# Two attention-convolution layers: the weight bands of layer 0 in one transfer per image, and the loads of x on another queue

## The chip, the cores and the metric

The kernel runs on one core of a Trainium2 chip. Its engines are TensorE (PE), VectorE (DVE), ScalarE (ACT), GpSimd (POOL) and SyncE (SP). SP and ACT each have a queue through which they issue DMA transfers; both queues feed the same 16 DMA engines. An engine works through its own instructions in order, and a DMA issue stands in that order like any other instruction: if it has to wait, everything behind it on that engine waits too. The metric is the device time of one execution in microseconds, as the median of several runs.

## The reference

The input x is 8 images of 56 x 56 pixels with 384 channels in float32. Two layers follow each other, each with a residual, and everything is float32.

```python
# layer 0, per image; gn = group norm with 32 groups, no affine part
xn = gn(x)
v = xn @ Wv.T                                       # 384 -> 384
a = (xn @ Wa.T).reshape(n, 12 heads, 9, 9)          # 384 -> 972
attn = softmax(a * 32 ** -0.5, axis=-1)
out[n, p, head] = sum over q of attn[n, head, p, q] * v[neighbour q of n, head]
y = fold(out)             # out[.., p] is added at neighbour p of its pixel
x = x + y @ Wo.T
# layer 1
xn = gn(x)
a = softmax((xn @ W_attn + b_attn).reshape(n, 6 heads, 9), axis=-1)
v = xn @ W_v + b_v
y[n, head] = sum over k of a[n, head, k] * v[neighbour k of n, head]
x = x + y @ W_proj + b_proj
```

Neighbours are the 3 x 3 pixels around one, and outside the image v is zero. In layer 0 each pixel gathers from 9 neighbours with 9 sets of weights and scatters the 9 results onto its neighbours, so altogether a pixel of y depends on the v of 5 x 5 pixels.

## The kernel before

Two images make a pair: R = 112 rows (both images' rows) lie on the partitions, and the work walks over the 56 columns. In layer 0 a step is one column of one pair, 224 steps in all, and a group is PX = 7 columns (NPX = 8 groups for each of 4 pairs).

What a step of layer 0 does. `attend` projects the column's normalised pixels to the 972 logits in three parts on TensorE, subtracts the maximum on DVE, takes the exponential on ACT (L491), sums and inverts on DVE, and normalises on POOL. It also projects v for a tile of 128 pixels, copies it on ACT (L498) and writes it to the table `vtab0` in DRAM through ACT's queue (`spread`, L296). `presum` and `fold` add up the weights that meet at the same pair of pixels, so that gathering and scattering together become one 5 x 5 stencil; `fold` copies the result (L555, L556) and writes it to one of three tables `ztab0` in DRAM through ACT's queue (L561).

The tables turn the stencil into matrix products. For a patch of 7 x 7 target pixels the 11 x 11 source pixels are the contraction, so 121 partitions. `rows_to_patches` (L361) reads v of these pixels from `vtab0` into `vp`, and `bands` (L308) reads the weights from `ztab0` into `z`, a tile of 128 partitions (source pixels) by 8 patches by 7 rows of targets. The table is skewed so that a plain strided read yields the matrix: row s of `z` begins a slot further on in the table, and where a source pixel is too far from a row of targets, the read meets the zeros with which the tables were filled before (`clear_weights`). For one image `z` is a band matrix: the first 48 source pixels reach only the first five of seven rows of targets, the last ones only the last four. `GROUPS0` (L88) splits the partitions into three ranges and gives each its rows of targets, and `bands` issues one transfer for each range. `z` is zeroed once at the start, so what no range reads stays zero. `contract` then multiplies `vp` and `z` on TensorE head by head and copies the result `pc` to `yT` on ACT (L600); `project_out` multiplies by Wo, adds the residual `xres`, and sends the result to DRAM.

The order of this work. `fetch_v` and `fetch` are called once for each group and issue the loads of `vp`, `z` and `xres` on SP; their contractions and projections go into a list of jobs that later steps run, from four steps on, two jobs a step. The order of TensorE's products is the order of the program, and a list scheduler of the compiler orders the other engines. Besides, `upkeep` runs in every step. It prepares the statistics of the next pair: `stats_load` reads four columns of x into `xr` (L392), `stats_chunk` transposes them on TensorE three steps later (L122), copies them on ACT (L409), takes sums on DVE and stores the transposed block to `xT` (L413). It also loads the transposed blocks of the present pair: `load` reads one into `xin` (L460), and four steps later `normed` normalises it on ACT (L471). `xr` and `xin` have two buffers each. The first pair's statistics come before all this, in a loop of their own at the start.

DMA completions are told by eight semaphores that the two queues share: a transfer that reuses one waits until that semaphore's last transfer has landed.

Layer 1 works in the same way with 3 x 3 stencils; its bands are read with `GROUPS1`, and its loads are issued by SP.

Of the kernel before, what the change touches and what calls it, by code (L numbers as in the profile page):

```python
# [15 lines left out]
def two_outlook_layers(  # L16
# [32 lines left out]
    nc = tc.nc  # L49

    B, H, W, C = x.shape
    P = 128
    NCH = C // P
    IMG = 2
    R = IMG * H
# [7 lines left out]
    XB = 4  # L63
# [21 lines left out]
    PY1, NPY1, SX1, SY1 = 8, 7, PX + 2, 10  # L85
    ROW1 = HEADS1 * PX

    GROUPS0 = (((0, 48), (0, 5)), ((48, 80), (0, 7)), ((80, P), (3, 7)))  # L88
    GROUPS1 = (((0, 45), (0, 5)), ((45, 90), (3, 8)))


# [8 lines left out]
    xf = x.rearrange("b y x c -> (b y) x c")  # L100
# [132 lines left out]
    def norm_params(st, name, params, key):  # L233

        mv = stat.tile([P, NCH, IMG, 2], F32, tag="mv", name=f"mv_{name}")

        def over_groups(src, what):
            pg = ps.tile([P, NCH, IMG], F32, tag="t", name=f"p{what}_{name}")
            for j in range(NCH):
                for i in range(NCH):  # L240
                    matmul(
                        pg[:, j, :], gmat[:, i, j * P : (j + 1) * P], src[:, i, :],
                        start=(i == 0), stop=(i == NCH - 1),
                    )
            g = stat.tile([P, NCH, IMG], F32, tag=what, name=f"{what}_{name}")
            nc.vector.tensor_copy(g, pg)
            return g

        for i in range(NCH):
            for b in range(IMG):  # L250
                nc.vector.bn_aggr(mv[:, i, b, :], st[:, i, b, :, :])
        yield
        mean = over_groups(mv[:, :, :, 0], "gmean")

        part = stat.tile([P, NCH, IMG], F32, tag="part", name=f"part_{name}")
        nc.vector.tensor_sub(part, mv[:, :, :, 0], mean)
        nc.vector.tensor_mul(part, part, part)
        nc.vector.tensor_add(part, part, mv[:, :, :, 1])
        yield
        var = over_groups(part, "gvar")  # L260
        std = stat.tile([P, NCH, IMG], F32, tag="std", name=f"std_{name}")
        nc.scalar.activation(std, var, AF.Sqrt, bias=eps_t)
        scale = const.tile([P, NCH, IMG], F32, name=f"scale_{name}")
        nc.vector.reciprocal(scale, std)
        bias = const.tile([P, NCH, IMG], F32, name=f"bias_{name}")
        nc.vector.scalar_tensor_tensor(bias, mean, -1.0, scale, ALU.mult, ALU.mult)
        params[key] = scale, bias
        yield
# [35 lines left out]
    def bands(queue, z, table, line, slot, row, top, groups, b, py, npy):  # L304

        for (s0, s1), (m0, m1) in groups:
            first = (b * H + top) * line + s0 * slot + m0 * row
            queue.dma_start(  # L308
                z[s0:s1, :, m0 * row : m1 * row],
                bass.AP(  # L310
                    table.tensor, table.offset + first + bands.at[row],
                    [[slot, s1 - s0], [py * line, npy], [1, (m1 - m0) * row]],
                ),
            )
# [65 lines left out]
    def layer0(late, pools):  # L380
# [5 lines left out]

        stats, st1s, params, xins, attns, pres, xrs, xts = {}, {}, {}, {}, {}, {}, {}, {}

        def stats_load(pair, blk):
            nm = f"{pair}_{blk}"  # L390
            xr = io.tile([P, XB, C], F32, tag="xr", name=f"xr_{nm}")[:R]
            nc.sync.dma_start(xr, xf[pair * R : (pair + 1) * R, blk * XB : (blk + 1) * XB, :])  # L392
            xrs[pair, blk] = xr

        def stats_chunk(pair, blk, i, alone):

            nm = f"{pair}_{blk}"
            if blk == 0 and i == 0:
                stats[pair] = stat.tile([P, NCH, IMG, NBLK, 6], F32, tag="st0", name=f"st0_{pair}")
            if i == 0:  # L400
                xts[pair, blk] = io.tile([P, NCH, XB, R], F32, tag="xt", name=f"xt_{nm}")
            xr, xt = xrs[pair, blk], xts[pair, blk]
            if alone:
                pt = bank(P, 0, XB * R).rearrange("p (m r) -> p m r", m=XB)
            else:
                pt = ps.tile([P, XB, R], F32, tag="t", name=f"pt_{nm}_{i}")
            for j in range(XB):
                transpose(pt[:, j, :], xr[:, j, i * P : (i + 1) * P], ident[:R, :R])
            nc.scalar.copy(xt[:, i], pt)  # L409
            for b in range(IMG):  # L410
                nc.vector.bn_stats(stats[pair][:, i, b, blk, :], xt[:, i, :, b * H : (b + 1) * H])
            if i == NCH - 1:
                nc.sync.dma_start(  # L413
                    xTs[pair][:, :, blk * XB * R : (blk + 1) * XB * R], xt.rearrange("p i m r -> p i (m r)")
                )
                del xrs[pair, blk], xts[pair, blk]

        stats_load(0, 0)
        for blk in range(NBLK):
            if blk + 1 < NBLK:  # L420
                stats_load(0, blk + 1)
            for i in range(NCH):
                stats_chunk(0, blk, i, True)
        for _ in norm_params(stats.pop(0), "0_0", params, 0):
# [32 lines left out]
        def load(g):  # L457
            pair, blk = divmod(g, NBLK)
            xins[g] = io.tile([P, NCH, XB, R], F32, tag="xin", name=f"xin_{g}")
            nc.sync.dma_start(  # L460
                xins[g].rearrange("p i m r -> p i (m r)"),
                xTs[pair][:, :, blk * XB * R : (blk + 1) * XB * R],
            )

        def normed(g):
            scale, bias = params[g // NBLK]
            xin, to = xins.pop(g), xn[:, :, g % 2 * XB : (g % 2 + 1) * XB, :]
            for i in range(NCH):
                for b in range(IMG):
                    rows = slice(b * H, (b + 1) * H)  # L470
                    nc.scalar.activation(  # L471
                        to[:, i, :, rows], xin[:, i, :, rows], AF.Identity,
                        bias=bias[:, i, b : b + 1], scale=scale[:, i, b : b + 1],
                    )
# [99 lines left out]
        def fetch(pair, px, due):  # L574
# [4 lines left out]
            for b in range(IMG):  # L579
                z, vp = zs[b], vps[b]  # L580
                bands(
                    nc.sync, z, ztab0[(pair * NPX + px) % NTAB], LINE0, SLOT0, ROW0, 0, GROUPS0,
                    b, PY0, NPY0,
# [67 lines left out]
        def upkeep(step):  # L651

            pair, c = divmod(step, W)
            while clearing and clearing[0][0] <= step:
                clearing.pop(0)[1]()
            if pair + 1 < NPAIR:
                blk, i = divmod(c - 3, NCH)
                if 0 <= c and i == 0 and blk < NBLK - 1:
                    stats_load(pair + 1, blk + 1)
                if 3 <= c and blk < NBLK:  # L660
                    stats_chunk(pair + 1, blk, i, False)
                elif NBLK * NCH + 3 <= c < NBLK * NCH + 6:
                    if c == NBLK * NCH + 3:
                        making["0"] = norm_params(stats.pop(pair + 1), f"0_{pair + 1}", params, pair + 1)
                    next(making["0"])
            g, j = divmod(step + XB + 2, XB)
            if j == 0 and g < NPAIR * NBLK:
                load(g)
            g, j = divmod(step + 2, XB)
            if j == 0 and g < NPAIR * NBLK:  # L670
                normed(g)

        load(0)
        load(1)
        normed(0)
        LAG = 3
        for step in range(NPAIR * W + LAG):
            if 2 <= step < NPAIR * W + 2:
                presum(*divmod(step - 2, W))
            todo = [lambda: jobs.run(step, 1)] * 2  # L680
            if step >= LAG:
                todo.insert(1, lambda: fold(*divmod(step - LAG, W)))
            between = lambda: todo.pop(0)() if todo else None
            if step < NPAIR * W:
                attend(*divmod(step, W), between)
                upkeep(step)
            while todo:
                between()

            pair, c = divmod(step - LAG - PX, W)  # L690
            if pair >= 0 and c % PX == 0:
                fetch_v(pair, c // PX)
            pair, c = divmod(step - LAG - PX - 1, W)
            if pair >= 0 and c % PX == 0:
                fetch(pair, c // PX, step + 4)
# [268 lines left out]
    with ExitStack() as late:  # L964
        with ExitStack() as pools:
            last_of_layer0 = layer0(late, pools)
        with ExitStack() as pools:
            layer1(pools, *last_of_layer0)
# [38 lines left out]
```

## Time and profile before

| | before |
|---|---|
| time, median of 3 runs | 3647.69 us (3647.13 to 3657.86) |
| span of the profiled execution | 3630.7 us |
| TensorE busy | 3460.3 us (95%) |
| ACT busy | 1166.5 us (32%) |
| DMA: queue of SP, queue of ACT (share of 16 engines' time) | 64.2%, 22.3% |
| DMA: bytes moved | 799.46 MB |
| bands of layer 0, transfers per image | 630 KB, 588 KB, 504 KB |

The profile is of one execution. A busy time is the time in which the engine ran instructions of the program; issuing a DMA does not count. Waits are inferred from semaphore events and are put down to the one that came last. A DMA share is the time that the transfers' packets took, over 16 engines; as packets can overlap, it can come out a little above 1. Layer 0 runs until about 2350 us and layer 1 from then on.

### The profile page before, as it was taken

The numbers are of one execution on the slowest core, as the hardware profiler recorded it, in microseconds if no ns is written. First come the engines' busy times: TensorE is split into PE (matmuls) and PEld (weight loads), VectorE is DVE, ScalarE is ACT, GpSimd is POOL, SyncE is SP. The second block draws the span as 40 slices with busy tenths as digits, with TensorE's granted clock in tenths as the row PEclk, the third lists the DMA queues.
The fourth block names the chain that finished last, engine by engine and source line by source line (L and its number), as shares of the span: only waits on it lengthen the run. The fifth ranks groups of instructions, "written<-read, shape, count | busy, mean of one in ns | idle before, by whom it ended". The sixth has DMA issues, their size and how long they took to land. (4 is left out here: it accounts for less than half of the span.)

```text
span 3630.7 us, 72464 instructions
## 1 busy us (share of the span) xinstructions
PE 3460.3 (95%) x29078; PEld 2374.7 (65%) x29078; DVE 1914.9 (53%) x4648; ACT 1166.5 (32%) x2727; POOL 982.6 (27%) x1409
## 2 busy tenths in 40 slices
PE   5999899999999999999999999979999999999998
PEld 4667676767777676767777776745656655556555
DVE  3766576666766676667766666723222323222322
ACT  3332232333233233332322232222434333434332
POOL 2544343433344333434433443410000000000000
PEclk9999999999999999999999999989999999999999
DMA  9799999989999889999888887897787878788876
GB/s 284 204 258 267 252 239 237 219 208 234 252 227 234 209 219 219 241 250 230 193 197 213 207 204 203 186 237 192 204 225 202 230 196 224 203 217 213 223 199 158
DMA packets 694302, 799.46 MB, mean 220 GB/s; under 512 B 304270, under 2 KB 647374, under 8 KB 689870
## 3 DMA queue, kind: packets, MB, share of 16 engines
q1 hardware_dynamic: 359438, 602.16, 64.2%
q10 hardware_dynamic: 334528, 192.66, 22.3%
q8 instruction: 229, 3.75, 0.5%
q14 instruction: 107, 0.88, 0.1%
HBM read 473.04 MB, written 321.66 MB: 219 GB/s over the span
## 5 line engine op out<-in xcount | busy, mean ns | idle before, releaser
L119 PE MATMUL bank<-wa_t,xn 128*112 128x288 f32 x4032 | 1089.1, 410 | 5.4 <-ACT xn L471 2.2
L119 PEld LDWEIGHTS bank<-wa_t,xn 128*112 128x112 f32 x4032 | 695.2, 178 | 257.5 <-issue 35.9
L510 POOL TENSOR_TENSOR at<-at,den 112x972 f32<-112x972 f32 x224 | 503.6, 2248 | 1235.3 <-DVE den L509 1192.5
L119 PE MATMUL po<-yT,wo_t 128*128 128x448 f32 (+1 forms) x2304 | 819.7, 495 | 5.4 <-DVE x1t L621 4.8
L119 PEld LDWEIGHTS po<-yT,wo_t 128*128 128x128 f32 x2304 | 433.6, 191 | 293.7 <-issue 189.3
L119 PE MATMUL pc<-z,vp 121*32 121x49 f32 (+1 forms) x17664 | 492.4, 255 | 63.8 <-issue 34.7
L119 PEld LDWEIGHTS pc<-z,vp 121*32 121x32 f32 (+1 forms) x17664 | 443.6, 131 | 145.2 <-issue 125.3
L119 PE MATMUL bank<-wc_t,xn 128*128 128x438 f32 x1176 | 483.5, 548 | 1.9 <-ACT xn L740 1.9
L486 DVE TENSOR_REDUCE mx<-bank 112x36 f32<-112x324 f32 x672 | 326.3, 485 | 290.0 <-PE bank L119 284.0
L119 PE MATMUL bank<-wv_t,xn 128*128 128x384 f32 x1176 | 417.6, 492 | 3.1 <-issue 1.5
L487 DVE TENSOR_TENSOR at<-bank,mx 112x324 f32<-112x324 f32 x672 | 329.1, 490 | 20.7
L491 ACT ACTIVATE at<-at 112x972 f32<-112x972 f32 x224 | 227.0, 1013 | 344.5 <-DVE at L487 314.0
L824 POOL TENSOR_TENSOR at<-at,den 112x378 f32<-112x378 f32 x32 | 30.2, 943 | 1118.0 <-DVE den L823 725.7
L119 PEld LDWEIGHTS bank<-wc_t,xn 128*128 128x128 f32 x1176 | 215.4, 193 | 173.5 <-issue 162.3
L740 ACT ACTIVATE xn<-x1t,bias,scale 128x168 f32<-128x168 f32 (+4 forms) x498 | 213.6, 503 | 330.2 <-DMA x1t<-x 251.9
L119 PEld LDWEIGHTS bank<-wv_t,xn 128*128 128x128 f32 x1176 | 218.9, 190 | 142.6 <-issue 19.5
L899 DVE SCALAR_TENSOR_TENSOR x1t<-po,bo_t,x1t 128x448 f32<-128x448 f32 (+1 forms) x192 | 120.2, 626 | 324.7 <-PE po L119 324.7
L533 POOL TENSOR_TENSOR pre<-at,at 112x108 f32<-112x108 f32 (+1 forms) x440 | 236.6, 538 | 150.4 <-DVE wt L556 136.0
L555 ACT COPY wt<-pw 112x120 f32<-112x120 f32 x224 | 58.1, 259 | 654.6 <-PE pw L119 570.5
L503 DVE TENSOR_TENSOR d<-at 112x432 f32<-112x432 f32 x224 | 141.3, 631 | 238.3 <-ACT at L491 238.0
L779 DVE TENSOR_TENSOR lgt<-bank,ba_t 128x54 f32<-128x54 f32 x196 | 41.2, 210 | 417.9 <-PE bank L119 414.6
L600 ACT COPY yT<-pc 128x294 f32<-128x294 f32 x256 | 103.8, 407 | 394.5 <-PE pc L119 353.6
(81 smaller groups left out, 2839.5 us busy)
## 6 DMA issues: line engine op xcount, KB each, us to landing
vp<-vtab SPq DMA_DIRECT2D x64, 1536.0 KB
ztab<-wt ACTq DMA_DIRECT2D x336, 183.8 KB
vp<-vtab SPq DMA_DIRECT2D x64, 945.0 KB
z<-ztab SPq DMA_DIRECT2D x64, 630.0 KB
xr<-in_x SPq DMA_DIRECT2D x56, 672.0 KB
xT<-xt SPq DMA_DIRECT2D x56, 672.0 KB
xin<-xT SPq DMA_DIRECT2D x56, 672.0 KB
xres<-xT SPq DMA_DIRECT2D x32, 1176.0 KB
```

Source lines behind the costliest of these rows:

```text
L119: tc.keep_in_program_order(nc.tensor.matmul(*args, **kwargs))
L486: nc.vector.tensor_reduce(mx[:, pi, :], pl.rearrange("r q a -> r a q"), AX.X, ALU.max)
L487: nc.vector.tensor_tensor(at[:, pi], pl, mx[:, pi, :].unsqueeze(1).to_broadcast([R, K2, PH]), ALU.subtract)
L491: nc.scalar.activation(at, at, AF.Exp, scale=SCALE0)
L503: nc.vector.tensor_add(d4, at[:, :, 0:4], at[:, :, 4:8])
L510: nc.gpsimd.tensor_tensor(at, at, den.unsqueeze(2).to_broadcast([R, K, K2, PH]), ALU.mult)
L533: nc.gpsimd.tensor_tensor(dst, terms[0], terms[1], ALU.add)
L555: nc.scalar.copy(mid[:, 0 : E0 : E0 - 1, :], pw[:, 0 : E0 : E0 - 1, :])
L600: nc.scalar.copy(yT[:, :, :, b, rows_of], pc.rearrange("p i n y m -> p i m (n y)"))
L740: nc.scalar.activation(to[:, i, :, rows], x1ts[g][:, i, lo - first : hi - first, rows], AF.Identity, bias=bias[:, i, b : b + 1], scale=sca ...
L779: nc.vector.tensor_add(staged[-1][1][:, len(staged[-1][0])], pa[:, :NA1], ba_t)
L899: nc.vector.scalar_tensor_tensor(res, po[:, :n], bo_t[:, j : j + 1], res, ALU.add, ALU.add)
```

## The change

Two things are changed in layer 0. `GROUPS0` becomes one range of all 128 partitions with all seven rows of targets, so that `bands` issues one transfer per image where it issued three. The transfer also reads positions that were left out before; there the table holds zeros. And the loads of x move from SP's queue to ACT's: `xr` for pairs 1 to 3 in `upkeep`, and `xin` for all pairs. The first pair's `xr` loads, at the start, stay on SP, and so do the stores of `xT` and the loads of `vp`, `z` and `xres`. The purpose is to read the bands with fewer transfers that span all partitions, and to take the loads of x out of the queue in which they stand behind the bands.

```diff
-    GROUPS0 = (((0, 48), (0, 5)), ((48, 80), (0, 7)), ((80, P), (3, 7)))
+    GROUPS0 = (((0, P), (0, 7)),)
...
-        def stats_load(pair, blk):
+        def stats_load(pair, blk, queue):
             nm = f"{pair}_{blk}"
             xr = io.tile([P, XB, C], F32, tag="xr", name=f"xr_{nm}")[:R]
-            nc.sync.dma_start(xr, xf[pair * R : (pair + 1) * R, blk * XB : (blk + 1) * XB, :])
+            queue.dma_start(xr, xf[pair * R : (pair + 1) * R, blk * XB : (blk + 1) * XB, :])
...
-        stats_load(0, 0)
+        stats_load(0, 0, nc.sync)
...
-                stats_load(0, blk + 1)
+                stats_load(0, blk + 1, nc.sync)
...
             xins[g] = io.tile([P, NCH, XB, R], F32, tag="xin", name=f"xin_{g}")
-            nc.sync.dma_start(
+            nc.scalar.dma_start(
                 xins[g].rearrange("p i m r -> p i (m r)"),
...
-                    stats_load(pair + 1, blk + 1)
+                    stats_load(pair + 1, blk + 1, nc.scalar)
```

## The prediction

> **What bounds the kernel now.** I read the page first, then busy time by stage, then what TensorE waits for, then SyncE's queue. The page:
>
> ```profile
> PE 3460.3 (95%) x29078; PEld 2374.7 (65%) x29078; DVE 1914.9 (53%) x4648; ACT 1166.5 (32%) x2727; POOL 982.6 (27%) x1409
> q1 hardware_dynamic: 359438, 602.16, 64.2%
> q10 hardware_dynamic: 334528, 192.66, 22.3%
> ```
>
> TensorE is busy 95% of the span, but the DMA engines are nearly full too: q1 (issued by SP) and q10 (by ACT) hold them for 86.5% of it. Either could set the time, so I look at stages. In the table by stretch, the columns are the stretch, its length, each engine's busy time with its count, the granted clock, the DMA share and GB/s:
>
> ```profile
> 100.00:2340.00 2240.00, 2195.83 (x19287) 1570.14 (x19286) 1503.20 (x3719) 683.31 (x1339) 909.69 (x1317) 0.99 0.91 225
> 2340.00:2520.00 180.00, 150.59 (x1407) 95.11 (x1405) 58.64 (x149) 47.16 (x120) 25.38 (x28) 0.91 0.83 204
> 2520.00:3631.00 1111.00, 1054.04 (x8135) 660.67 (x8133) 310.67 (x660) 402.57 (x1208) 28.30 (x30) 0.99 0.80 209
> ```
>
> The change touches layer 0, the first row. TensorE idles there for 2240 - 2195.8 = 44 us and no more. Transfers can win only those 44 us and the slow clock that follows an idle stretch. The waits of TensorE in that stretch (total us, times, longest):
>
> ```profile
> PE pt L122 <- DMA xr<-in_x: 21.7, 3, 11.8
> PE pc L119 <- issue: 12.0, 13, 1.5
> PE pc L119 <- DMA z<-ztab: 2.7, 1, 2.7
> PE bank L119 <- ACT v L498: 1.6, 1, 1.6
> ```
>
> Half of the idle time is three waits for an `xr` load. Why it comes late is seen in SP's queue before the longest of them (start, duration):
>
> ```profile
> 398.79 23.61 SPq L308 DMA_DIRECT2D z<-ztab  x6
> 423.12 0.57 SPq L609 DMA_DIRECT2D xres<-xT  x1
> 423.74 0.62 SPq L631 DMA_DIRECT2D x<-x1t  x1
> 424.46 0.88 SPq L392 DMA_DIRECT2D xr<-in_x  x1
> ```
>
> The load stands behind six band transfers whose issues, with their waits, take 23.6 us, and goes out at 424.5; TensorE waits from 427.5 to 439.3. In the other two cases it goes out at 804.8 and 1386.6, and TensorE resumes at 812.5 and 1393.9. After each, the clock is at half for a while:
>
> ```profile
> 439.30:445.30 6.00, 6.00 (x106) 4.49 (x106) 1.68 (x4) 3.85 (x8) 0.00 (x0) 0.50 0.74 241
> 812.50:817.40 4.90, 4.87 (x58) 3.41 (x62) 1.53 (x4) 0.53 (x1) 1.18 (x4) 0.50 1.04 305
> 1393.90:1397.60 3.70, 3.70 (x10) 2.34 (x10) 0.69 (x2) 0.53 (x1) 0.00 (x0) 0.50 1.01 299
> ```
>
> [...]
>
> ```profile
> 1066.00:1084.00 18.00, 18.00 (x82) 13.33 (x81) 14.54 (x39) 4.50 (x9) 8.77 (x13) 1.00 1.05 176
> 1038.00:1052.00 14.00, 14.00 (x59) 8.86 (x52) 9.21 (x23) 3.50 (x6) 4.10 (x6) 1.00 1.01 301
> ```
>
> The first stretch is mostly band transfers, the second mostly `vp` loads of 128 partitions. Both fill the engines (share 1.05 and 1.01), yet the bands move 176 GB/s and `vp` 301. [...] what I count on is not bandwidth, it is that a load no longer stands behind another queue's waits.
>
> **The bands.** Removed: per image three transfers of 630 + 588 + 504 KB = 1722 KB; added: one of 128 x 8 rows x 2352 B = 2352 KB. The positions outside the old ranges are zeros of the table. A group has two images. Before: 3.53 MB at 176 GB/s = 20.0 us of full engines. After: 4.82 MB, at `vp`'s 301 GB/s 16.0 us; if the rate stayed at 176, 27.4 us. I take 16.0, since partitions and rows are shaped like `vp`'s; 27.4 is the other bound. A group lasts about 70 us (its first band issues at 995.2, the next group's at 1065.1). So the DMA share goes from 0.91 to about 0.91 - 4.0/70 = 0.85, or at worst to 0.91 + 7.4/70 = 1.02. This is not on the path itself: TensorE waits for bands once in layer 0, 2.7 us, at the first group. After that wait the clock is at 0.62 for 4.5 us (201.9 to 206.4), 1.7 us lost. With one issue instead of three and a quicker transfer I drop both: -4.4 us.
>
> SP also issues 128 fewer transfers (64 images x 2) at 0.44 us, 56 us of queue, and each has a wait of its own ahead of it: `z` <- `ztab` is SP's largest wait (433 us, 58 times). TensorE doesn't wait for SP's issue itself, so I count this as nothing further.
>
> **The loads of x.** 42 `xr` loads (pairs 1 to 3) and 56 `xin` loads go to ACT. Removed are the 21.7 us of waits and the half clock after them: (6.0 + 4.9 + 3.7) us at 0.5 = 7.3 us. Together -29.0 us. An `xr` load is due three columns ahead of its use, over 20 us, and took 15, 8 and 7 us from issue to use in the three cases; issued on time it arrives on time.
>
> Added on ACT: 42 x 0.35 + 56 x 0.57 us (medians of the two issues on SP) = 47 us of queue. ACT is busy 683 us of 2240, so this lies in its idle time. Queued behind such an issue are the copies of `pt`, `pc`, `pw` and the exponential; DVE waits for the exponential, TensorE for the copies. ACT already waits 12 times for a `vtab` transfer ahead of L555 (55.6 us, longest 5.3), while TensorE's waits on ACT come to 1.6 us: holds of about 5 us are absorbed. An issue can also be slow[...] (longest 1.7 us for `xr`, 6.8 for `xin`). For the few holds beyond the cushion I charge +5 us; the bounds are 0 and the inherited waits of the first rival. ACT's own buffer waits vanish: the 60 us that SP spent on L460 for ACT's use of `xin` become program order.
>
> **Short issue gaps.** The 12.0 us in 13 gaps inside `pc` have no releaser in the profile. I take -2 for emptier DMA engines, with bounds -12 and +12.
>
> Sum: -29.0 - 4.4 - 2 + 5 = about -30. From 3647.7: 3618 us.
>
> **Rivals.**
> ACT becomes the place of the wait. On SP the two loads waited 30 times for `ztab` or `vtab` transfers (L392 47.5 + 31.0, L460 32.8 + 22.2 = 133 us, mean 4.4, longest 11.5). If ACT inherits these ahead of its copies, and half of the time passes through to TensorE with some 10 us of slow clock, it costs 77 us and gives 3618 - 5 + 77 = about 3690; a quarter passing gives about 3650. For it: ACT's queue is in order, and its work is on TensorE's loop. Against: its idle 70%, and the waits of this size absorbed now. Likelier than 3690 is something like 3670.
>
> The DMA engines become the bound: the band rate stays at 176 GB/s, the share reaches 1.02, some 1.4 us of each 70 us group is exposed (32 x 1.4 = 45 us), the `xr` gain stays: about 3647 - 33 + 45 = 3659. For it: 40 MB more in a stage at 0.91. Against: the 301 GB/s of the same shape.
>
> The gain is hidden: a load issued on time stops TensorE less, but the next wait (bands, issue gaps, ACT) takes the place, and a third of the gain is left: about 3638, within the bound of no change. For it: TensorE's order is fixed, and time won early can be lost at the next late transfer. Against: the waits for bands in layer 0 are one, of 2.7 us.
>
> **How the numbers follow.** Forecast 0.66; hidden 0.16; ACT 0.12; DMA bound 0.06. Faster by over 0.3% means under 3636.7: the forecast and a fourth of the hidden case, 0.70. Slower means over 3658.7: most of the ACT case and over half of the DMA case, 0.15. Same 0.15. Low end: all of the 44 us of idle time and 9 us of slow clock won would give 3595, so 3594. High end 3660 leaves out only the bad ACT cases.
>
> **What would show it.** Right: no wait of `pt` for `xr`; the bands' stretch near 300 GB/s; the DMA share of layer 0 lower though it moves 40 MB more; ACT's issue waits up, TensorE's waits on ACT still a few us; TensorE idle in layer 0 near 15 us. Wrong: TensorE waiting for `xn`, `yT` or `v` copies (first rival), a share near 1 with waits on `z` or `vp` (second), or the same idle time under other names (third). The order in which the compiler puts the loads into ACT's queue isn't in the profile; if it puts them late, the `xr` waits stay.

## The result and the profile after

The changed kernel takes 3612.8 us (median of 4, 3605.08 to 3615.88) against 3651.64 us before in the same comparison: ratio 0.9889, 95% interval 0.9865 to 0.9913. Forecast were 3618 us from 3647.7, a ratio of 0.992. The amount is about right; the division of it between the two edits was wrong, as the experiments will show.

The page of the changed kernel, the lines that answer to those of before:

```profile
PE 3460.6 (96%) x29078; PEld 2375.8 (66%) x29078; DVE 1914.9 (53%) x4648; ACT 1165.1 (32%) x2727; POOL 986.4 (27%) x1409
...
q1 hardware_dynamic: 329614, 576.00, 51.1%
q10 hardware_dynamic: 362304, 260.11, 27.5%
```

TensorE's work is unchanged. The DMA engines move 41 MB more and are held for less time: q1 and q10 together 78.6% of the span instead of 86.5%.

To compare by stage I cut each run at two landmarks that every trace has: the first logits product of layer 0, and the 3.9 us gap of TensorE ahead of the second-last `pw` of layer 0. Between them all kernels run the same 19512 recorded products. Columns: stretch, length, busy time and count of each engine, clock, DMA share, GB/s. Before:

```profile
0.00:87.10 87.10, 46.91 (x210) 40.02 (x211) 34.69 (x105) 25.60 (x48) 19.23 (x34) 1.00 0.91 287
87.10:2364.50 2277.40, 2233.22 (x19512) 1596.38 (x19512) 1528.68 (x3779) 696.63 (x1362) 918.70 (x1331) 0.99 0.91 224
2364.50:3630.70 1266.20, 1180.13 (x9360) 738.29 (x9356) 351.50 (x765) 444.27 (x1318) 44.67 (x44) 0.98 0.80 209
```

After:

```profile
0.00:95.70 95.70, 46.95 (x211) 40.07 (x211) 35.12 (x105) 25.73 (x48) 19.27 (x34) 0.60 0.94 296
95.70:2331.30 2235.60, 2223.84 (x19512) 1591.56 (x19512) 1529.03 (x3779) 693.62 (x1362) 922.42 (x1331) 1.00 0.80 245
2331.30:3610.80 1279.50, 1189.79 (x9357) 744.21 (x9356) 350.76 (x765) 445.73 (x1318) 44.73 (x44) 0.97 0.78 206
```

The start is 8.6 us longer, the stage of layer 0 is 41.8 us shorter, the rest 13.3 us longer. In the stage, TensorE's idle time falls from 44.2 to 11.8 us (length less busy time), and its busy time by 9.4 us, near the 9.0 us of slow clock after waits that the prediction had counted (7.3 and 1.7). The rest is layer 1 with its transition, whose code is the same; over the 12 profiles of kernels that leave it alone, the one before included, it lies between 1255.9 and 1286.3 us, so its 13 us can't be put down to the change. The two profiled executions differ by 19.9 us where the medians differ by 38.8: the one of the kernel before took 3632.65 us, 15 us less than that kernel's median. The waits of TensorE in layer 0 after the change (100 to 2320 us; total, times, longest):

```profile
PE pc L119 <- ACT yT L600: 7.3, 2, 3.7
PE pw L119 <- POOL pre L531: 2.9, 4, 1.3
PE pc L119 <- issue: 1.3, 1, 1.3
```

No wait for `xr` or `z` is left, the unexplained gaps inside `pc` fell from 12.0 to 1.3 us, and there are two waits for ACT's copies. A stretch full of band transfers, like the one at 176 GB/s before:

```profile
1051.00:1065.00 14.00, 14.00 (x64) 10.32 (x63) 10.94 (x30) 3.83 (x7) 6.71 (x12) 1.00 1.04 384
```

At the same full share (1.04) the engines now move 384 GB/s.

### The profile page after: what moved, and what is told of

Its sections match the earlier page's. It is cut to its first block, busy times and chain, and to the rows that moved or that the text cites. A ratio compares the mean times of both kernels' runs of the same rounds, so it can differ in the third digit from the quotient of the medians.

```text
span 3610.8 us, 72232 instructions
## 1 busy us (share of the span) xinstructions
PE 3460.6 (96%) x29078; PEld 2375.8 (66%) x29078; DVE 1914.9 (53%) x4648; ACT 1165.1 (32%) x2727; POOL 986.4 (27%) x1409
## 4 chain that ended last, share of the span: by engine, by line
PE 78%; DMA 16%; DVE 2%; ACT 1%; issue 1%; POOL 1%; ACTq 0%; SPq 0%; POOLq 0%; DVEq 0%
PE bank L119 44%; PE po L119 15%; PE pc L119 11%; DMA ztab<-wz 5%; PE pw L119 4%; DMA z<-ztab 3%; DMA lgtab<-lgt 2%; PE pt L122 2%; DMA at<-lgtab 1%; DMA xr<-in_x 1%; PE bank L122 1%; DMA vtab<-v 1%; DMA x1t<-x 1%; DMA xT<-xt 1%; DMA vp<-vtab 1%
```

## The experiments

Each kernel was compared with the one before on the same chip. Chips differ (medians of the kernel before: 3625.5 us for the first four, 3647.3 for the next four, then 3661.0 and 3648.8), so ratios are compared, and stages of profiles.

A stage is read from one execution, and it varies. Four of the kernels below have the same layer 0, the one of the bands alone, with its instructions in the same order on every engine; their stages take 2236.6, 2238.0, 2248.4 and 2250.3 us. So two stages that differ by less than some 14 us show nothing by that alone.

### Bands alone

The kernel before with one line changed:

```diff
-    GROUPS0 = (((0, 48), (0, 5)), ((48, 80), (0, 7)), ((80, P), (3, 7)))
+    GROUPS0 = (((0, P), (0, 7)),)
```

> One transfer of 128 partitions per image, all loads of x still on SP. Theory A (the xr load's place in SP's queue cost the 29 us): the waits of pt for xr stay near 20 us, layer 0 after its statistics takes 2265 to 2277 us (2277.4 before, 2235.6 with the whole change), the time is 0.995 to 1.000 of before. Rival B (the bands themselves held the queue: two quick issues instead of six slow ones let every later load out in time): the xr waits fall under 5 us without moving a load, the stage takes 2235 to 2250 us, the time is 0.988 to 0.993. Both expect the DMA share of the stage near 0.80, as with the whole change[...].

Measured: 0.9884 (0.9860 to 0.9909), as good as the whole change. The stage:

```profile
87.30:2323.90 2236.60, 2224.75 (x19512) 1591.39 (x19512) 1527.88 (x3780) 695.52 (x1362) 919.07 (x1331) 1.00 0.78 247
```

Two lines of SP's waits in layer 0, before and then with the bands alone:

```profile
SPq L308 <- DMA ztab<-wt: 433.1, 58, 19.9
...
SPq L392 <- PE pt L122: 74.3, 13, 11.8
```

```profile
SPq L392 <- PE pt L122: 187.1, 26, 16.9
...
SPq L308 <- DMA ztab<-wt: 168.7, 33, 7.7
```

Rival B holds and my theory falls: the `xr` waits are gone although every load of x still stands in SP's queue. SP's wait at the bands (L308) for the table's writes is 169 us where it was 433 us, the longest 7.7 instead of 19.9. SP now comes to the `xr` load early enough to wait mostly for the buffer to be free (`PE pt`, 187 us where it was 74): the load is ahead of its use.

### Loads alone, and xr alone

The whole change with the old `GROUPS0`; then also with `xin` back on SP (`nc.sync.dma_start` in `load`).

> The old three ranges of bands, xr and xin on ACT. Theory A: no wait of pt for xr, the stage takes 2240 to 2252 us, the time is 0.990 to 0.994 of before, though the DMA share stays near 0.91. Rival B: the DMA engines are still full and SP's queue still slow, so the time is lost at other waits (z, vp, ACT's copies) and stays at 0.997 or more; with ACT taking over waits for ztab and vtab, TensorE's waits on ACT's results exceed 15 us.

> The old three ranges; only xr on ACT, xin back on SP. Theory A: as much as both loads together, 0.990 to 0.994, for TensorE waited for xr alone and never for xin. Rival B: no gain, 0.997 or more. If xin on ACT was what mattered (it frees 56 issues of SP), this one stays at 0.997 and the run with both loads gains.

Measured: 0.9971 (0.9954 to 0.9989) and 0.9952 (0.9929 to 0.9975). The first is where rival B put it, the second where neither theory did. The stage with both loads moved:

```profile
0.00:95.10 95.10, 46.46 (x210) 39.93 (x211) 35.03 (x105) 25.62 (x48) 19.26 (x34) 0.59 0.91 295
95.10:2342.80 2247.70, 2227.85 (x19512) 1592.01 (x19512) 1529.41 (x3779) 694.40 (x1362) 919.76 (x1331) 1.00 0.89 225
```

In the stage theory A's size comes out: 29.7 us less than before in both kernels, no `xr` wait, and from 100 us on TensorE's waits for ACT's results are none and 3.1 us, far from the 15 of the rival. That it agrees with the forecast to the microsecond is luck, given how far stages vary. And only a part shows in the time. With `xin` on ACT the start takes 8 us more, 95.1 us. Of the 29.7 us (0.8%), less 8 us for the first kernel, 0.3 and 0.5% were measured; what takes the remaining 0.3% isn't settled, since the rest of these runs (1271.0 and 1278.2 us) lies within the spread of unchanged code.

### Bands in halves of 64 partitions, loads on ACT

```diff
+    GROUPS0 = (((0, 64), (0, 7)), ((64, P), (0, 7)))
```

> The whole change, but the bands in two transfers of 64 partitions each (0 to 63 and 64 to 127), all rows of targets: the same bytes and packets of 2352 B. [...] Theory A: packets of the bands slow down to near twice their 95 ns, the DMA share of the stage rises from 0.80 to 0.95 or more, and the stage takes 2250 us or more as the engines are full. Rival (the number of transfers or the longer rows[...], made the bands quicker): the share stays at 0.80 to 0.83 and the time within 0.2% of the changed kernel's 0.989.

Measured: 0.9980 (0.9967 to 0.9993). From the packet records of the stage I work out a mean of 166 ns for the bands' packets of 2352 B, against 105 ns in the changed kernel: 1.6 times, where the "near twice" of the expectation was an estimate. The stage takes 2249.5 us at a share of 0.91, not the 0.95 expected, and the limit of 2250 us is missed by half a microsecond. The time is that of the loads alone with the old bands (0.9971), not that of the whole change (0.9889): with the bands in halves, what quick bands add is gone.

### Partitions against the number of issues, all loads on SP

Three transfers of 128 partitions by rows of targets, and two of 64 partitions with all rows. Both move the bytes of the change. Theory P puts the gain down to the partitions that a transfer spans, theory N to the number of issues.

```diff
+    GROUPS0 = (((0, P), (0, 3)), ((0, P), (3, 5)), ((0, P), (5, 7)))
...
+    GROUPS0 = (((0, 64), (0, 7)), ((64, P), (0, 7)))
```

> All loads on SP; bands of all 128 partitions but in three transfers by rows of targets (0 to 2, 3 and 4, 5 and 6): the bytes of the change[...], as many issues as before. Theory P ([...]quick bands let SP's queue go on): nearly as good as one transfer, the stage of layer 0 takes 2245 to 2258 us, the waits of pt for xr stay under 6 us, the time is 0.988 to 0.992 of before. Theory N (the number of issues, each with its own wait, held the queue): the xr waits stay at 15 us or more, the stage takes over 2265 us, the time is 0.995 or more.

> All loads on SP; bands in two transfers of 64 partitions each with all rows: the bytes of the change[...], one issue fewer than before. Theory P: packets of 2352 B near 170 ns as in the run of halves with the loads on ACT, share of the stage 0.91 or more, stage 2280 to 2310 us, time 0.998 to 1.008 of before. Theory N: the stage gains some 15 us from the issue saved, 2265 us or less, time under 0.995.

Measured: 0.9898 (0.9868 to 0.9927) for three transfers over all partitions, 0.9997 (0.9980 to 1.0014) for two over half of them. Their stages, in this order:

```profile
87.40:2337.30 2249.90, 2227.58 (x19512) 1591.98 (x19512) 1525.21 (x3779) 692.84 (x1362) 918.69 (x1331) 1.00 0.84 245
```

```profile
87.20:2367.30 2280.10, 2237.78 (x19512) 1596.38 (x19512) 1528.61 (x3779) 695.89 (x1362) 919.61 (x1331) 0.99 0.92 241
```

And a stretch of the second that is mostly bands, with the waits of TensorE in its layer 0:

```profile
1439.00:1453.00 14.00, 14.00 (x61) 10.05 (x60) 10.62 (x27) 2.59 (x6) 7.48 (x12) 1.00 1.03 213
```

```profile
PE pc L119 <- issue: 17.7, 20, 2.8
PE pt L122 <- DMA xr<-in_x: 8.6, 1, 8.6
PE po L119 <- DVE x1t L621: 5.3, 1, 5.3
```

This decides it for the partitions that a transfer spans. Three issues over all partitions give the gain; fewer issues over half of the partitions give none. The full engines move 213 GB/s in this stretch and 384 GB/s in that of the changed kernel; both also hold a few other transfers. With the halves the `xr` wait is smaller than before (8.6 us against 21.7), yet other waits fill the time, such as the gaps inside `pc` (17.7 us against 12.0).

Packets of the same 2352 B take 182 ns (mean of the stage) in the old middle range of 32 partitions, 166 and 167 ns in the halves of 64, and 102 to 105 ns over all 128. From 32 to 64 partitions little changes; from 64 to 128 much does. What makes the difference was not shown. The only ranges of 64 partitions that were run are 0 to 63 and 64 to 127.

### Bands and xr, and the whole change once more

The first is the change with `xin` left on SP.

> The change without its xin part: one transfer of bands, xr on ACT, xin on SP. If xin on ACT delays the start (in the runs with it ACT waits from 14.8 to 24.2 us for a store of xT, ahead of the copies of the statistics), the first matmul of layer 0 begins at 87 to 88 us instead of 95 to 96, the stage takes about 2245 us, and the time is about 0.986 to 0.988 of before. If the late start is chance or comes from xr, it stays at 95.

> The changed kernel again, to stand beside the others on the same chip. If the loads add nothing once the bands are quick and cost 8 us at the start, it is 0.2% slower than the kernel with bands and xr: 0.989 to 0.991 of before, start at 95 us. Layer 1 took 1270 us in its first profile against 1253 before; if that comes from the change it is again over 1262, if it is chance it lies between 1245 and 1262.

Measured: 0.9888 (0.9863 to 0.9914) and 0.9899 (0.9869 to 0.9929); for the first 0.986 to 0.988 had been expected. The first starts its stage at 88.9 us, the second at 95.0; the stages take 2238.4 and 2232.7 us. So the late start belongs to `xin` on ACT. Over all profiles it is 95.0 to 95.7 us in the five with `xin` on ACT and 87.1 to 88.9 us in the nine others. The difference in time is within the intervals. Where the start goes, in the changed kernel, is seen in SP's and ACT's queues:

```profile
13.08 0.61 SPq L413 DMA_DIRECT2D xT<-xt  x1
13.79 2.71 SPq L392 DMA_DIRECT2D xr<-in_x  x1
```

```profile
24.15 0.64 ACTq L460 DMA_DIRECT2D xin<-xT  x1
27.36 0.53 ACT L409 COPY xt<-bank 128x448 f32<-128x448 f32 x1 [12.07 <-PE bank L122]
```

TensorE's waits for `xr` in the start, before and then after:

```profile
PE bank L122 <- DMA xr<-in_x: 29.0, 11, 5.0
```

```profile
PE bank L122 <- DMA xr<-in_x: 35.0, 11, 11.6
```

The compiler put the first two `xin` loads among the copies of the statistics, where the first waits until 24.1 us for a store of `xT`; in the kernel before, SP issued them at 68 us. It changed SP's own order as well: a store of `xT` (13.08 us) now goes ahead of an `xr` load (13.79), which before went out at 12.51 us. At that load TensorE waits 11.6 us, until 26.3 us, and 4.2 us before. This one wait is nearly all of the delay: it is 11.0 to 12.0 us in the five profiles with `xin` on ACT and 4.1 to 5.3 us in the nine others. ACT's hold was over at 24.1 us, before the load landed, so the wait that ends last is that for the load, in SP's changed order. Why the load takes so long to land, with the store ahead of it, no run isolates.

### A wait of layer 1 moved to GpSimd

Bands alone, and the read of the logits in `regroup` issued by GpSimd:

```diff
-            nc.sync.dma_start(
+            nc.gpsimd.dma_start(
                 lgs[g].rearrange("r m k h -> r m (k h)"),
```

> One transfer of bands, all loads of x on SP, and in layer 1 the read of the logits table (L804) issued by GpSimd, which is idle there, instead of SP, which waits 343 us at it for the write to land, with vp and the bands of layer 1 queued behind. If SP's queue holds layer 1 as it held layer 0, TensorE's waits for z and POOL there (17.6 + 18.3 us with the bands alone) fall by 15 us or more with the slow clock after them, and the time is 0.981 to 0.985 of before. If layer 1's waits come from the landing of the weights' own writes, the time stays at that of the bands alone.

Measured: 1.0166 (1.0127 to 1.0204), slower. TensorE's waits from 2330 us on, in the second run of the bands alone and then here:

```profile
PE pc L119 <- DMA z<-ztab: 23.0, 11, 3.5
PE pw L119 <- POOL at L824: 22.4, 15, 3.0
```

```profile
PE pw L119 <- POOL at L824: 117.1, 28, 9.5
PE pc L119 <- ACT yT L883: 19.9, 10, 5.4
...
PE pc L119 <- DMA z<-ztab: 6.0, 5, 3.6
```

Half of the expectation came: the waits for `z` fell to 6.0 us. But the read itself is on the path. Its median from issue to landing is 6.2 us here and 3.0 us from SP (in the second run of the bands alone), DVE waits 219.7 us for it instead of 101.0, and TensorE at the end of this chain 117.1 us instead of 22.4. The place in the queue is not what delays it: counted from the issue of the write, the read goes out after 4.4 us here and 4.2 us from SP (means). The wait that blocked SP was cheaper than a later landing of what it waited to read.

### Bands alone against the whole change on one chip

> The bands alone again, to stand beside the whole change and the GpSimd variant on one chip. If the moved loads are worth nothing beside quick bands and cost the 8 us start, this is 0.2 to 0.4% faster than the whole change; if they help, it is slower than it.

> The whole change again on the same chip: 0.989 to 0.990 of before, start at 95 us, layer 1 at 1262 to 1272 us as in both its earlier profiles if that is its own, at 1245 to 1262 if chance.

Measured: 0.9856 (0.9822 to 0.9889; 3609.9 us) and 0.9890 (0.9857 to 0.9923; 3619.8 us). The medians differ by 9.9 us, 0.3%, in favour of the bands alone; the intervals overlap. Start and stage: 87.5 and 2238.0 us against 95.4 and 2239.9 us. The rest took 1282.1 and 1283.2 us, so that stretch is no mark of the whole change.

### The same in layer 1

Bands alone, with layer 1's two ranges made one:

```diff
-    GROUPS1 = (((0, 45), (0, 5)), ((45, 90), (3, 8)))
+    GROUPS1 = (((0, 90), (0, 8)),)
```

> The bands alone, and in layer 1 also one transfer per image in place of two: all 90 partitions with all eight rows of targets, 529 KB become 945 KB less the narrower type of nothing (90 x 7 x 1344 B = 827 KB). [...] Theory P: nothing, 0.985 to 0.989 of before as with the bands of layer 0 alone, layer 1 at 1246 to 1275 us as in the other runs, its DMA share unchanged or up by 0.01 to 0.02. If fewer issues or longer rows are worth something by themselves, layer 1 takes under 1240 us and the time is under 0.983.

Of the two sizes in that text 827 KB is the one meant; in the same unit the two old transfers have 517 KB. Measured: 1.0001 (0.9983 to 1.0019): the whole gain of layer 0 is gone again. The landmarks show layer 0's stage at 2250.3 us and the rest at 1318.4 us, 32 us over the highest of the runs with layer 1 unchanged. TensorE's waits there, and the bands of layer 1 in the first run of the bands alone and then here (KB each, median us from issue to landing):

```profile
PE pc L119 <- DMA z<-ztab: 53.0, 21, 5.6
PE pw L119 <- POOL at L824: 26.9, 15, 5.3
```

```profile
z<-ztab SPq DMA_DIRECT2D x128, 258.4 KB, 6.1
```

```profile
z<-ztab SPq DMA_DIRECT2D x64, 826.9 KB, 9.2
```

The wait for `z` was 23.0 us in the second run of the bands alone. One transfer of 827 KB lands after 9.2 us, where the two of 258 KB had a median of 6.1 us. Not "nothing" but a loss: in layer 1 TensorE already waits for the landing, so the later landing is paid for at once, with 53.0 us of waits in place of 23.0. That nothing would change was an estimate of mine, and it left out the landing that ends TensorE's wait.

## Why the prediction was right, and where not

**What bounds the kernel.** Right. TensorE bounds layer 0, the gain could come only from its 44 us of idle time and the clock, and it did: idle down by 32.4 us, busy time by 9.4.

**The loads of x.** The size was right: -29.0 us forecast, -29.7 in the stage with the loads or `xr` alone. That this is what the change does was wrong. With quick bands nothing that the loads add stands out (stages of 2235.6, 2232.7 and 2239.9 us with them, 2238.4 with `xr` alone, 2236.6 to 2250.3 in four without), and in time the bands alone are as good. The two edits cure the same wait and do not add up. That the total came near is luck in this sense: the forecast credited one edit with the wait that the other removes as well.

**The bands.** The step that failed is "This is not on the path itself", with the sentence that SP's saved waits count "as nothing further". I credited 4.4 us to the bands; alone they bring 27 to 41 us of stage. I had shown the chain myself: before the longest wait, the `xr` load stood behind six band issues of 23.6 us. I read it as a matter of which queue the load is in, and not of why those issues took so long. In the other two waits the load was not even right behind bands: SP stood 7.4 and 7.9 us at the load itself, by the profile for a write of `vtab` to land.

The halves and the three transfers by rows show that what counts is how long full engines are held, and not the number of issues: two issues over 64 partitions each win nothing at a share of 0.92 (0.9997 of the time before), three over all 128 win at 0.84 (0.9898). The likeliest link is that the table's writes land earlier on emptier engines (share 0.78 with the bands alone, 0.91 before) and so release SP. The packet records show its first half. In ACT's queue, 560 packets of 336 B are one write of `ztab` in layer 0. Taken in order, from its issue to its last packet it takes a median of 6.2 us before, 7.1 with the halves and all loads on SP, 5.4 with three transfers by rows, and 4.5 and 5.0 in the two runs of the bands alone. That this releases SP in time is argued: SP's wait at L308 for these writes fell from 433 to 169 us with the bands alone, but with the halves too, to 254 us, without a gain. No run isolates it.

**Sizes.** The rate of the new bands was taken from `vp` as 301 GB/s and is 384; the DMA share went to 0.80, not 0.85. The issue gaps were forecast to shrink by 2 us and shrank by 10.7; in the four profiles of the bands alone 5.3 to 10.0 us of them are left. For ACT I charged 5 us; TensorE's waits on its copies are 7.3 us.

**What was not foreseen.** The 8 us at the start. The text said that the compiler's order of loads in ACT's queue isn't in the profile, but looked for harm only in layer 0's steady part.

**The rivals.** That ACT became the place of the wait isn't shown. TensorE's waits on ACT's copies rose from 1.6 to 7.3 us, but ahead of both of them ACT stood idle for 6.5 us with issues of its own writes of `vtab` next in line, and with three transfers by rows, where no load is on ACT, such waits come to 12.5 us. The DMA bound did not come, as the rate rose from 176 to 384 GB/s. The gain was not hidden.

## What to carry to other kernels

When DMA engines are full, read GB/s beside the share: two stretches at share 1.04 and 1.05 differed here by a factor of two (384 and 176 GB/s), and at equal rows of 2352 B the slow one (213 against 384) was that of transfers over 64 of the 128 partitions. Spanning all partitions paid here even with 37% more bytes (0.9884 of the time before, with the bands alone). When a load is late in a queue, ask first why what stands ahead of it is slow; moving the load and speeding up what it waits behind cured the same wait here (21.7 us for `xr` before, none with either edit), and their gains should not be added up. Where TensorE already waited for the landing of a transfer, as in layer 1, more bytes or a longer way to landing cost time at once: landing after 9.2 us for 6.1, TensorE waited 53.0 us for `z` and not 23.0; with the read of the logits landing after 6.2 us for 3.0, it waited 117.1 us at `pw` and not 22.4.

## What was not expected of the hardware

The short gaps inside runs of `pc` products, without a releaser in the profile, do not follow the DMA share alone. They come to 12.0 us at a share of 0.91 before and 17.7 at 0.92 with the halves and all loads on SP, but to 4.7 at 0.91 with the halves and the loads on ACT; at 0.78 to 0.80 they come to 1.2 to 3.7 us with `xr` on ACT and to 5.3 to 10.0 with all loads on SP. What they wait for isn't in the trace. Three transfers of rows of 672 and 1008 B over all partitions held the engines for 0.84 of the stage, two of 2352 B rows over half of them for 0.92: here the number of partitions weighed more than the length of the rows.
